# Two expert tiles held back for the last mixing, its norms' halves set side by side, and four steps' exponentials per sum product in the first and last attention

## The chip, the cores and the metric

The kernel runs on 1 core of one Trainium2 chip. The metric is the device time of one execution in microseconds (us), as a median of several. The engines are PE (TensorE: matrix products and transposes), DVE (VectorE), ACT (ScalarE), POOL (GpSimd) and SP (SyncE, which issues most DMAs). Each runs its instructions in the order in which the kernel issued them to it.

## The reference, cut to what matters

One layer for x of shape (4, 256, 32, 32): 4 images, 256 channels, N = 1024 pixels each. A mixing part (`conv`) is followed by a mixture-of-experts part (`ffn`), both added to their input.

```python
def conv(x):                                  # per image
    xn = layernorm(x over channels)
    xm = mamba(4 groups of 64 channels) + skip * xn     # selective scan over N
    g  = sigmoid(conv1d(xm));  R = conv1d(conv1d(g * xm)) + g * xm
    xm2 = conv1d(conv1d(cat(x, R))) + x
    x_local  = conv1d_depthwise(xm2)
    q, k, v  = xm2 @ inw                      # 8 heads of 32
    att = softmax(q @ k.T / sqrt(32))         # 1024 x 1024 per head
    x_global = (att @ v) @ outw
    y  = gelu(layernorm(cat(x_local, x_global) @ fc_w))     # norm "lgn"
    y  = depthwise3x3(layernorm over the pixels(y))         # 9 taps
    return layernorm(y over channels) @ proj_w              # norm "fin"
x = x + conv(ln_c(x))
t = tokens(x)                                 # 4096 x 256
p = top-2 softmax gate(ln_t(t) @ Wg)          # 8 experts
t = t + sum_e p_e * (gelu(ln_t(t) @ W1[e]) @ W2[e])   # 256 -> 1024 -> 256
```

The softmax needs, for each head and query, the sum of the exponentials over all 1024 keys. The norms `lgn` and `fin` need, for each pixel, a mean over the 256 channels.

## The kernel before, in words

**Two parts, one program.** `network()` (lines 73 to 1340) holds the mixing of all four images, the class `Experts` (1352 to 1916) the rest. The order of all work on all engines is written by hand. Each strand of work is a Python generator; `start` puts it among the running ones, `beat` (L1235) advances the tick by one and resumes each strand whose tick has come, and what a strand yields is the number of ticks until its next turn. `until` beats until a flag is set, `drain` until no strand is left. So the yields do not make anything wait on the chip; they fix in which order instructions of different strands stand in each engine's queue. On the chip an instruction waits for the engine's earlier ones and for its operands.

**Images 0 to 2.** The selective scan of an image goes in steps (L592 to 607): a product and a scan on DVE, a product on POOL, sums on PE, 16 steps for each of two halves of N and four groups. The other work of image b-1 (convolutions, attention, joining, norms) and of image b-2 (3x3 taps, final norm, routing) is issued among the scan steps of image b. When the attention of image b-1 starts, no scan step is issued until that attention is three steps from its end (the flag `attended`).

**Image 3.** After the last scan step come, in this order, with expert tiles as filler between: the convolutions of image 3 (L741 on) beside taps, final norm and routing of image 2; the attention of image 3, with no tile beside it (`hold`, L1320); then joining, norms, taps, routing of image 3 with tiles beside it; then the last series of tiles alone.

**Expert tiles.** A tile is 256 rows of one expert's queue, taken through both products. Tiles are sorted into series by which images must have been routed: 8 of image 0 and 1, 8 when image 2 is routed too, 23 when all are; 35 of these 39 run here, the last four only on demand. A tile: a gathered load of its rows `xs` (L1786, SP queue), transposes `xp` (L1832, PE) and a copy `xT` (L1833, DVE), four h steps (products L1855, PE, and two gelus L1860, ACT, each), four y steps (products L1865, PE), then an add of its rows into Y in memory (L1881, POOL queue). The generator `tiles()` (L1148) yields `T["pace"]` ticks after each of the eight steps, 1 if nothing set it. The weights of a tile (2 MB) are loaded two tiles ahead by SP. The first tile of a series also needs the series' table (L1669 to 1740, 22 small operations on DVE). `PACE` (L1273) holds the ticks per tile step for the stages of image 3: joining's products 4, norms 2.2, taps 0.9, routing 2; they are set by `pace()` (L995) only for image 3. While image 3's convolutions run, the pace is 1.

**Attention** (L899 to 982). Four blocks per image (two groups of four heads, two halves of the queries), each of eight steps `kt` of 128 keys. A step: four products of logits `st` (L918, PE, into PSUM), one step ahead of use; four exponentials `e` (L928, ACT, 128 x 512); four products `av` with the values (L960, PE). On odd steps DVE adds the step's four exponentials to those of the step before (L970), and `sum_pair` (L935) sums the pair's rows by four products with ones, behind the next step's `av`. `end_block` (L942) takes the sums' logarithm and its negative exponential on ACT and multiplies on DVE; it is issued in the next block's first odd step, and behind the last step.

**Norms** (`inverse_deviation`, L1000). Per half of the pixels: squares on ACT, a mean over channels on PE (`column_mean`, L371), a root as Ln and Exp on ACT (L355, L356), then one multiplication per channel half on DVE (L1018). ACT's Ln and Exp share one table of functions, gelu and sigmoid need others; a change loads a table (1283 ns in the rows of this profile). `joined` (L1021) calls it for `lgn` behind the products ao and fc, and closes with a gelu; `around` (L1060) has the statistics over pixels, a root, and the 16 taps on DVE (L1097); `sent_off` (L1103) subtracts the means, calls it for `fin`, has the products pr, and routes (`dispatch`, L1503: gate, places in the queues L1567, blank rows written from the ACT queue L1450, rows scattered into XS from the POOL queue L1628).

Of the kernel before, what the change touches and what calls it, by code (L numbers as in the profile page):

```python
# [21 lines left out]
NHEAD, HD = 8, 32  # L22
# [50 lines left out]
def network(  # L73
# [29 lines left out]
    B = x.shape[0]  # L103
# [25 lines left out]
    eps5 = cpool.tile([P, 1], F32, name="eps5")  # L129
# [14 lines left out]
    with tc.tile_pool(name="w_conv", bufs=1) as wp, tc.tile_pool(  # L144
        name="act8", bufs=8
    ) as act8, tc.tile_pool(name="act4", bufs=7) as act4, tc.tile_pool(
        name="act2", bufs=17
    ) as act2, tc.tile_pool(name="steps", bufs=2) as actd, tc.tile_pool(
        name="steps4", bufs=6
    ) as acts, tc.tile_pool(name="rows", bufs=3) as actc, tc.tile_pool(  # L150
        name="small", bufs=1
    ) as small, tc.tile_pool(
        name="spread", bufs=2, space=bass.MemoryType.DRAM
# [107 lines left out]
        ones = experts.every  # L261
# [80 lines left out]
        def half(h):  # L342
            return ts(h, HALF)
# [8 lines left out]
        def root(r, var, eps, scale=1.0):  # L352

            log_exp()
            nc.scalar.activation(r, var, AF.Ln, bias=eps, scale=scale)  # L355
            nc.scalar.activation(r, r, AF.Exp, scale=-0.5)  # L356
# [10 lines left out]
        def column_mean(name, chunks):  # L367

            out = ps(name)
            for ci, chunk in enumerate(chunks):  # L370
                nc.tensor.matmul(  # L371
                    out, ones_mean, chunk, start=(ci == 0), stop=(ci == len(chunks) - 1)
                )
            return out
# [110 lines left out]
        T = {}  # L485
# [374 lines left out]
        NK = N // P  # L860
# [38 lines left out]
        def attention(b):  # L899

            v8, qk = QKV.pop(b)
            rows = [
                largest(b, g, qk[g][:, 0, :], qk[g][:, 1, :]) if shifted else None
                for g in range(2)
            ]
            yield 1
            steps = [(g, h, kt) for g in range(2) for h in range(2) for kt in range(NK)]  # L910

            def logits(g, h, kt):

                q, k = qk[g][:, 0, :], qk[g][:, 1, :]
                sts = [ps(f"st_{b}_{g}_{h}_{kt}_{i}") for i in range(4)]
                for i in range(4):
                    r = ts(i, HD)
                    nc.tensor.matmul(  # L918
                        sts[i], k[r, ts(kt, P)], q[r, half(h)], start=True, stop=not shifted
                    )  # L920
                    if shifted:
                        nc.tensor.matmul(
                            sts[i], ones[HD * i : HD * i + 1, :],
                            rows[g][HD * i : HD * i + 1, half(h)], start=False, stop=True,
                        )
                es = [a2(f"e_{b}_{g}_{h}_{kt}_{i}") for i in range(4)]
                for i in range(4):
                    nc.scalar.activation(es[i], sts[i], AF.Exp, scale=1.0 / HD**0.5)  # L928
                return es

            log_exp()
            ahead = logits(*steps[0])
            pairs, accs, ending = [], [None, None], []

            def sum_pair():  # L935
                kt, acc, es = pairs.pop()
                for i in range(4):
                    nc.tensor.matmul(
                        acc[ts(i, HD)], ones[:, 0:HD], es[i], start=(kt == 1), stop=(kt == NK - 1)
                    )  # L940

            def end_block(g, h, values, total):  # L942

                low, out = a2(f"low_{b}_{g}_{h}"), OT[b][g][:, half(h)]
                at = (2 * b + g) * 2 + h
                keep = [None, None] if shifted else [sums[:, i, at : at + 1] for i in range(2)]
                nc.scalar.activation(low, total, AF.Copy, accum_out=keep[0])
                nc.scalar.activation(low, low, AF.Ln, bias=added)
                nc.scalar.activation(low, low, AF.Exp, scale=-1.0, accum_out=keep[1])
                nc.vector.tensor_tensor(out, values, low, ALU.mult)  # L950

            for at, (g, h, kt) in enumerate(steps):
                es = ahead
                if at + 1 < len(steps):
                    ahead = logits(*steps[at + 1])
                if kt == 0:

                    accs = [ps(f"av_{b}_{g}_{h}_{w}") for w in range(2)]
                for i in range(4):
                    nc.tensor.matmul(  # L960
                        accs[0][ts(i, HD)], v8[:, kt, ts(4 * g + i, HD)], es[i],
                        start=(kt == 0), stop=(kt == NK - 1),
                    )
                if pairs:
                    sum_pair()
                if kt % 2 == 0:
                    first = es
                else:
                    for i in range(4):
                        nc.vector.tensor_tensor(first[i], first[i], es[i], ALU.add)  # L970
                    pairs.append((kt, accs[1], first))
                    if ending:
                        end_block(*ending.pop())
                if kt == NK - 1:
                    ending.append((g, h, *accs))
                if at == len(steps) - 3:
                    T["attended", b] = True
                yield 1
            sum_pair()
            yield 1  # L980
            end_block(*ending.pop())
            yield 1
# [14 lines left out]
            if b == B - 1:  # L997
                T["pace",] = ticks

        def inverse_deviation(name, xc):  # L1000
            r = a4(f"r_{name}")

            def squares(h):
                sq = [a2(f"sq_{name}_{h}_{c}") for c in range(NC2)]
                for c in range(NC2):
                    nc.scalar.activation(sq[c], xc[:, c, half(h)], AF.Square)
                return sq

            for h in range(2):
                sq = squares(h)  # L1010
                yield 1
                var = column_mean(f"var_{name}_{h}", sq)
                yield 2
                root(r[:, half(h)], var, eps5)
                yield 1
            yield 1
            for c in range(NC2):
                nc.vector.tensor_tensor(xc[:, c, :], xc[:, c, :], r, ALU.mult)  # L1018
                yield 1

        def joined(b):  # L1021

            xloc, oT = XLOC.pop(b), OT.pop(b)
            pace(b, PACE["product"])
            xglo = a8(f"xglo_{b}")
            T["attending", b] = True
            yield from in_turn(
                CO_H, lambda at: product(
                    f"ao_{b}_{at[0]}_{at[1]}", aoutT_s, at[0],
                    [oT[ci][:, half(at[1])] for ci in range(NC2)],  # L1030
                ),
                lambda at, r: nc.scalar.activation(
                    xglo[:, at[0], half(at[1])], r, AF.Identity, bias=ob[:, at[0] : at[0] + 1]
                ),
            )

            xc = XC[b] = a8(f"xc_{b}")
            both = (xloc, xglo)
            yield from in_turn(
                CO_H, lambda at: product(  # L1040
                    f"fc_{b}_{at[0]}_{at[1]}", fcT_s, at[0],
                    [both[ci // 2][:, ci % 2, half(at[1])] for ci in range(4)],
                ),
                lambda at, r: nc.scalar.activation(
                    xc[:, at[0], half(at[1])], r, AF.Identity, bias=fcb[:, at[0] : at[0] + 1]
                ),
            )

            T["joining", b] = True
            pace(b, PACE["norm"])  # L1050
            yield from inverse_deviation(f"lgn_{b}", xc)
            for c in range(NC2):
                nc.scalar.activation(
                    xc[:, c, :], xc[:, c, :], AF.Gelu, bias=col("lgn_b", c), scale=col("lgn_w", c)
                )
            loaded[0] = None
            log_exp()
            yield 2

        def around(b):  # L1060
# [17 lines left out]
            xz = []  # L1078
            pace(b, PACE["taps"])
            for c in range(NC2):  # L1080
# [22 lines left out]
        def sent_off(b):  # L1103

            xc = XC.pop(b)
# [12 lines left out]
                lambda h: column_mean(f"mean_{b}_{h}", [xc[:, c, half(h)] for c in range(NC2)]),  # L1118
                centre,
            )  # L1120
            yield from inverse_deviation(f"fin_{b}", xc)

            def residual(at, r):
                co, h = at
# [139 lines left out]
        def until(*flag):  # L1264
            while not T.get(flag):
                beat()
# [3 lines left out]

        PARTS = 2 * NB

        PACE = {"product": 4, "norm": 2.2, "taps": 0.9, "routing": 2, "rows": 0.75}  # L1273
        with tc.manual_schedule(engines=ALL):
            log_exp()
            start(weights(), first_normalised())
# [2 lines left out]
            for b in range(B):  # L1279
                for p in range(PARTS):  # L1280
                    at = b * PARTS + p
                    stop = b > 0 and p == PARTS // 2 - 1 or at == len(parts) - 1
# [33 lines left out]
                flagged(convolutions(B - 1), "convolved"),  # L1316
                one_by_one(around(B - 2), sent_off(B - 2)),
            )
            until("convolved")
            T["hold",] = True  # L1320
            until("held")
            start(flagged(attention(B - 1), "attended", B - 1, 2), local(B - 1))
# [29 lines left out]
class Experts:  # L1352
# [11 lines left out]
    T = 256  # L1364
# [649 lines left out]
```

## Time and profile before

| | us |
|---|---|
| median of three runs | 2473.78 (2473.77 to 2481.73) |
| the profiled execution | 2480.27 |
| its span (first to last instruction) | 2478.3 |
| PE busy, share of the span | 2131.6 (86%) |
| DVE busy | 1631.0 (66%) |
| ACT busy | 1196.3 (48%) |
| POOL busy | 1101.3 (44%) |
| mean granted clock of PE in the span | 0.909 |
| attention of image 0 (506 to 618 us): PE, DVE, ACT busy | 109.6, 70.8, 85.2 of 112 |
| end of the last tile to the end (2441 to 2478.3 us): PE busy | 11.8 of 37.3 |

How to read it: times on the axis are microseconds from the start of the span of one profiled execution. "Busy" is time in which an engine executes instructions other than register, branch, semaphore and DMA-issuing ones; matrix products are pipelined and their ends are modelled, so a fully busy PE need not be at its peak. The granted clock is the share of full speed that the throttle allowed PE. In a line of a timeline the number in brackets is the idle time ahead of an instruction and `<-` what ended it; `xs<-XS` reads "xs, made from XS"; `x8` counts instructions.

A product 512 columns wide stands as two records in PE's counts: 1024 records of `st` are the 512 products of four images.

### The profile page before, as it was taken

The page shows a single profiled execution, that of the slowest core. Times are in us where ns is not written, and L with a number is a line of the kernel's source. Part 1 is how long each engine was busy: PE and PEld are TensorE (multiplying, and loading weights), DVE is VectorE, ACT ScalarE, POOL GpSimd, SP SyncE. Part 2 cuts the span into 40 slices and gives each one's busy share as a digit, 9 for nine tenths or more (in the row PEclk, how much of TensorE's full clock was granted, in tenths as well). Part 3 has the DMA queues.
Part 4 walks back from the last instruction along what each step waited for, and adds up shares of the span by engine and source line. Part 5 has one row for each costly group of instructions (what it writes and reads, how often), then busy time and mean ns, then how long its engine had stood idle before and what let it go on. Part 6 is the DMA issues. An engine that isn't in the chain of part 4 may idle for free. (4 is left out here: it accounts for less than half of the span.)

```text
span 2478.3 us, 28314 instructions
## 1 busy us (share of the span) xinstructions
PE 2131.6 (86%) x8810; PEld 947.8 (38%) x8810; DVE 1631.0 (66%) x2255; ACT 1196.3 (48%) x2020; POOL 1101.3 (44%) x1182
## 2 busy tenths in 40 slices
PE   7777768999978799987689999568999978899995
PEld 2111112322211132222113223115672456788885
DVE  3978998866898978789888787984425254211111
ACT  4554445568655448764264786324238542122221
POOL 0767776622676850465866115561131011322221
PEclk7978988999998899988788999779999988899998
DMA  3534343220343330133422102343330144666665
GB/s 89 140 96 107 95 103 80 58 57 26 77 100 98 74 74 26 35 104 91 124 61 59 46 22 69 88 147 105 112 109 16 58 134 133 194 196 191 195 198 156
DMA packets 154981, 244.31 MB, mean 99 GB/s; under 512 B 34184, under 2 KB 103452, under 8 KB 154816
## 3 DMA queue, kind: packets, MB, share of 16 engines
q1 hardware_dynamic: 135640, 217.05, 30.9%
q0 software_dynamic: 13264, 17.85, 3.7%
q10 hardware_dynamic: 5912, 7.45, 0.9%
q8 instruction: 74, 1.21, 0.2%
q14 instruction: 91, 0.75, 0.1%
HBM read 141.16 MB, written 33.98 MB: 71 GB/s over the span
## 5 line engine op out<-in xcount | busy, mean ns | idle before, releaser
L607 POOL TENSOR_TENSOR hs<-hs,cs 128x512 f32<-128x512 f32 x512 | 670.5, 1311 | 212.2 <-DVE hs L602 166.8
L613 PE MATMUL yp<-hs,quads 128*32 128x512 f32 x1024 | 345.8, 695 | 161.2 <-POOL hs L607 118.9
L588 ACT ACTIVATE dA<-dts,A 128x512 f32<-128x512 f32 x512 | 342.5, 713 | 277.6 <-DMA dts<-dt 189.8
L595 DVE TENSOR_TENSOR dBu<-dts,bs 128x512 f32<-128x512 f32 x512 | 347.7, 679 | 69.6 <-PE bs L580 17.6
L1881 POOL DMA_INDIRECT Y<-ys,dest x70 | 111.0, 1585 | 592.8 <-DVE ys L1875 586.4
L602 DVE TENSOR_TENSOR_SCAN hs<-dA,last,dBu 128x512 f32<-128x512 f32 x256 | 327.6, 1280 | 24.9 <-DVE dBu L595 0.5
L602 DVE TENSOR_TENSOR_SCAN hs<-dA,dBu 128x512 f32<-128x512 f32 x256 | 312.4, 1220 | 31.3 <-ACT dA L588 6.2
L1860 ACT ACTIVATE hs<-h,b 128x256 f32<-128x256 f32 x280 | 117.0, 471 | 398.8 <-PE h L1855 211.3
L928 ACT ACTIVATE e<-st 128x512 f32<-128x512 f32 x512 | 263.2, 606 | 84.8 <-PE st L918 84.5
L1865 PE MATMUL y<-w,hs 128*128 128x256 f32 x1120 | 270.2, 394 | 12.3 <-ACT hs L1860 12.3
L1855 PE MATMUL h<-xT,w 128*128 128x256 f32 x1120 | 254.4, 383 | 1.2 <-DVE xT L1833 1.2
L1865 PEld LDWEIGHTS y<-w,hs 128*128 128x128 f32 x1120 | 219.7, 199 | 55.0 <-ACT hs L1860 14.4
L1833 DVE COPY xT<-xp 128x512 f32<-128x512 f32 x35 | 24.2, 691 | 323.8 <-PE xp L1832 323.7
L606 POOL COPY last<-hs 128x1 f32<-128x1 f32 x256 | 66.9, 261 | 371.8 <-DVE hs L602 340.7
L1855 PEld LDWEIGHTS h<-xT,w 128*128 128x128 f32 x1120 | 214.1, 192 | 41.3 <-issue 10.7
L580 PE MATMUL bs<-u,xpwT_s 128*32 128x512 f32 x1024 | 177.9, 674 | 43.9 <-DVE hs L602 23.8
L613 PEld LDWEIGHTS yp<-hs,quads 128*32 128x32 f32 x1024 | 55.7, 119 | 414.2 <-POOL hs L607 280.8
L970 DVE TENSOR_TENSOR e<-e,e 128x512 f32<-128x512 f32 x256 | 171.2, 730 | 54.1 <-ACT e L928 29.9
L918 PE MATMUL st<-qk 32*128 32x512 f32 x1024 | 193.1, 653 | 6.8 <-DVE hs L602 4.5
L496 PE MATMUL up<-xn,inwk 64*128 64x512 f32 x256 | 138.8, 688 | 11.5 <-DVE hs L602 11.4
L960 PE MATMUL av<-e,v 128*32 128x512 f32 x1024 | 142.6, 621 | 0.0
L918 PEld LDWEIGHTS st<-qk 32*128 32x128 f32 x1024 | 67.6, 187 | 131.9 <-issue 87.6
(273 smaller groups left out, 2511.8 us busy)
## 6 DMA issues: line engine op xcount, KB each, us to landing
w<-in_W_dram SPq DMA_DIRECT2D x136, 512.0 KB
dts<-dt SPq DMA_DIRECT2D x512, 128.0 KB
cs<-cd SPq DMA_DIRECT2D x512, 64.0 KB
xs<-XS SPq DMA_DIRECT2D x35, 260.0 KB
b<-in_b_dram SPq DMA_DIRECT2D x35, 128.0 KB
xn<-in_x_dram SPq DMA_DIRECT2D x8, 512.0 KB
XL<-xl SPq DMA_DIRECT2D x8, 512.0 KB
xl<-XL SPq DMA_DIRECT2D x4, 1024.0 KB
```

The source lines that it names most:

```text
L580: nc.tensor.matmul(bs[r], xpwT_s[:, n, s : s + 1].to_broadcast([P, 32]), T[b, n, "u"][:, half(h)], start=True, stop=True,)
L588: nc.scalar.activation(dA, T[b, n, h, "dts", g][:, 0, :], AF.Exp, scale=A[:, g, n, q : q + 1])
L595: nc.vector.tensor_tensor(dBu, T[b, n, h, "dts", g][:, 1, :], T[b, n, h, "bs", q], ALU.mult)
L602: nc.vector.tensor_tensor_scan(hs, T[b, n, h, "dA", i], dBu, 0.0 if h == 0 else last, ALU.mult, ALU.add)
L607: nc.gpsimd.tensor_tensor(hs, hs, T[b, n, h, "cs", q], ALU.mult)
L613: nc.tensor.matmul(T[b, n, h, "yp"][ts(g, 32)], quads, T[b, n, h, "hs", q * GD + g], start=(q == 0), stop=(q == GS - 1),)
L918: nc.tensor.matmul(sts[i], k[r, ts(kt, P)], q[r, half(h)], start=True, stop=not shifted)
L928: nc.scalar.activation(es[i], sts[i], AF.Exp, scale=1.0 / HD**0.5)
L960: nc.tensor.matmul(accs[0][ts(i, HD)], v8[:, kt, ts(4 * g + i, HD)], es[i], start=(kt == 0), stop=(kt == NK - 1),)
L970: nc.vector.tensor_tensor(first[i], first[i], es[i], ALU.add)
L1855: nc.tensor.matmul(hp[:, i, :], w1(c, k), xT[:, c, :], start=(c == 0), stop=(c == NC2 - 1))
L1865: nc.tensor.matmul(yp[:, ts(t, C)], hs[:, k, ts(t, P)], w2(k), start=(k == 0), stop=(k == NHC - 1))
```

## The change

In the attention of the first and the last image, DVE adds the exponentials of four steps rather than two before one sum product of them, so that a block has two groups of four sum products rather than four; `end_block` keeps its place in the block's step 1. In `inverse_deviation` for image 3 (`alone`), the squares of both halves are issued first, then both column means, then both roots, with a yield ahead of each of these four; for the other images nothing moves. Finally the paces of the tiles for image 3 change, and two are new: 1.6 while image 3's convolutions run (1 before, unset) and 1 again from there to the joining.

```diff
+            many = 4 if b in (0, B - 1) else 2
             def sum_pair():
                 kt, acc, es = pairs.pop()
                 for i in range(4):
                     nc.tensor.matmul(
-                        acc[ts(i, HD)], ones[:, 0:HD], es[i], start=(kt == 1), stop=(kt == NK - 1)
+                        acc[ts(i, HD)], ones[:, 0:HD], es[i], start=(kt < many),
+                        stop=(kt == NK - 1),
                     )
...
-                if kt % 2 == 0:
+                if kt % many == 0:
                     first = es
                 else:
                     for i in range(4):
                         nc.vector.tensor_tensor(first[i], first[i], es[i], ALU.add)
-                    pairs.append((kt, accs[1], first))
-                    if ending:
-                        end_block(*ending.pop())
+                    if kt % many == many - 1:
+                        pairs.append((kt, accs[1], first))
+                if kt == 1 and ending:
+                    end_block(*ending.pop())
...
-        def inverse_deviation(name, xc):
+        def inverse_deviation(name, xc, alone):
             r = a4(f"r_{name}")
...
-            for h in range(2):
-                sq = squares(h)
-                yield 1
-                var = column_mean(f"var_{name}_{h}", sq)
-                yield 2
-                root(r[:, half(h)], var, eps5)
-                yield 1
-            yield 1
+            if alone:
+                sq = [squares(h) for h in range(2)]
+                var = []
+                for h in range(2):
+                    yield 1
+                    var.append(column_mean(f"var_{name}_{h}", sq[h]))
+                for h in range(2):
+                    yield 1
+                    root(r[:, half(h)], var[h], eps5)
+            else:
+                for h in range(2):
+                    sq = squares(h)
+                    yield 1
+                    var = column_mean(f"var_{name}_{h}", sq)
+                    yield 2
+                    root(r[:, half(h)], var, eps5)
+                    yield 1
+                yield 1
...
-            yield from inverse_deviation(f"lgn_{b}", xc)
+            yield from inverse_deviation(f"lgn_{b}", xc, b == B - 1)
...
-            yield from inverse_deviation(f"fin_{b}", xc)
+            yield from inverse_deviation(f"fin_{b}", xc, b == B - 1)
...
-        PACE = {"product": 4, "norm": 2.2, "taps": 0.9, "routing": 2, "rows": 0.75}
+        PACE = {
+            "convolutions": 1.6, "product": 2, "norm": 1.2, "taps": 0.67, "routing": 1.3, "rows": 1
+        }
...
                 one_by_one(around(B - 2), sent_off(B - 2)),
             )
+            T["pace",] = PACE["convolutions"]
             until("convolved")
+            T["pace",] = 1
             T["hold",] = True
             until("held")
```

## The prediction

> **What bounds the kernel now.** I read the 40 slices first, then the busy times by stage, then the engines in order of time where the change acts.
>
> ```profile
> PE   7777768999978799987689999568999978899995
> DVE  3978998866898978789888787984425254211111
> PEclk7978988999998899988788999779999988899998
> ```
>
> A slice is 62 us. DVE carries the scans until slice 27 (1662 us); from there it falls to 2 to 5 and PE carries the time. The stages from 1662 us on (columns: stretch, length, busy PE, PEld, DVE, ACT and POOL with instruction counts, granted clock, DMA share, GB/s):
>
> ```profile
> 1662.00:1735.00 73.00, 65.13 (x220) 39.51 (x221) 40.31 (x56) 38.39 (x52) 11.64 (x13) 0.91 0.40 125
> 1735.00:1854.00 119.00, 119.00 (x496) 86.91 (x494) 41.14 (x118) 32.97 (x64) 24.32 (x33) 1.00 0.38 114
> 1854.00:1942.00 88.00, 88.00 (x642) 26.12 (x643) 47.92 (x74) 73.60 (x146) 10.41 (x15) 1.00 0.06 13
> 1942.00:2099.00 157.00, 136.29 (x504) 98.14 (x503) 64.16 (x165) 61.51 (x101) 18.95 (x19) 0.89 0.38 115
> 2099.00:2165.00 66.00, 51.59 (x231) 44.31 (x230) 12.08 (x43) 11.64 (x28) 27.23 (x40) 0.89 0.70 204
> 2165.00:2441.00 276.00, 275.92 (x1310) 242.56 (x1310) 48.34 (x153) 63.81 (x152) 61.00 (x57) 0.99 0.63 180
> ```
>
> They are: convolutions of image 3 up to its rp products; from there to its attention; its attention; its joining, norms, 3x3 taps and routing; the last held tiles; 19 tiles of the last series. PE is full in the second, third and last, and idles or runs slowly (clock 0.89) in the others. An expert tile costs PE 14.25 us (the transposes xp come every 14.25 us, 2129.56 and 2143.82); that is 8 steps of 1.72 us (8 records of 128x256) and 0.44 us of xp. A 512-wide matmul is two records and costs 0.86 us.
>
> So the time from 1662 to 2165 us is PE work plus PE's losses. Stage 1: 20 tile steps (34.4), 3 xp (1.3), 24 wide matmuls (20.6) = 56 of 72 us, loss 16. Stage 2: 64 us of tiles and 56 of convolutions, routing and projections = 120, no loss. Stage 4 to the places product (2087 us): 45 of dense products and 9.5 half tiles (68) = 113 of 146, loss 33. From there to the xp at 2165 us: 58 of 78, loss 20.
>
> **Two tiles held back.** The order of the two programs shows 7 tiles ahead of attention 3 before and 5 after; at image 3's places product both are at the 12th. Stage 1 loses 8 tile steps, stage 2 one half tile of h and one of y. Stage 2 is full, so it pays 13.8 + 0.4 = 14 us. Stage 1 I followed hop by hop with the durations of its rows: taps of image 2 end at 1691 (one xT copy less), two means and a y step to 1695.5, four gp to 1699; then on ACT sigmoid 1.27, table 1.28, squares 1.15, table, sigmoid, table, root 1.32, table, gelu 0.84, the first depthwise start (1.22) at about 1709 where it was 1723.3; squares, a gelu, the second start to 1717; two DVE passes of 1.28 to 1719.6; rp. It was 1735.6: 16 us. Together 30. The routing and the d4r passes behind rp have fewer tiles to hide under, and I saw no slack check there; I take **-24**. Ends: -14 (only the full stage pays) and -30.
>
> **Where they go.** Stage 4 takes 28.5 us of PE work more. Again hop by hop, from the end of attention, against before's clock times. Three more steps ahead of var_lgn, less a wait of 2.6 us: +3. The norm's "one round trip" is not one on ACT: in the new order a tile's gelu stands ahead of the first root and another between the two, with a table load on each side (1.28 + 0.84 + 1.28 + 1.32 = 4.7 us per half), and the first gelu waits for an h step put behind var_lgn_1. The roots end at 1990 instead of 1982.7: +7.5. Then the bn of the second half stands on DVE behind an xT copy, that behind xp, that behind a y step whose last gelu comes at 1998; and the 22 small DVE operations of the second series' table (4.2 us; before at 1944.6, beside ao) now stand just ahead of the first tap. Taps start +9.5, end +11.6 (2034.8). In the final norm all squares and both roots do stand together, one table load: its multiplication ends +7. Products, rows and gate have 1.5 half tiles more: places +13 (2100).
>
> Behind places it comes back. Before, the eight blank-row DMAs stand on ACT between the 2nd and 3rd gelu of a tile, and PE waits for the third:
>
> ```profile
> 2099.61 10.24 ACTq L1450 DMA_DIRECT2D XS<-blank  x8
> ...
> 2100.81 1.89 PE L1865 MATMUL y<-w,hs 128*128 128x256 f32 x8
> 2110.43 3.78 PE L1865 MATMUL y<-w,hs 128*128 128x256 f32 x8 [7.73 <-ACT hs L1860]
> 2114.01 1.06 PE L1832 MATMUL xp<-ident,xs 128*128 128x128 f32 x4
> 2114.86 4.50 PE L1865 MATMUL y<-w,hs 128*128 128x256 f32 x16
> ...
> 2154.61 3.62 PE L1865 MATMUL y<-w,hs 128*128 128x256 f32 x16
> 2164.91 1.11 PE L1832 MATMUL xp<-ident,xs 128*128 128x128 f32 x4 [6.68 <-DMA xs<-XS]
> ```
>
> After, they stand behind the tile's fourth gelu, and PE has a y half and the next h half (14 us) to run under their 10.2: the 7.7 us go, and 2.8 us of slow matmuls behind them (3.78 for 1.89, 4.50 for 3.62, all that followed to 2119). The 6.7 us before the last series' first xp stay: the table, its register load and the SP queue behind it are ordered as before; POOL's last rows now stand behind the same tile's adds. My sum: xp at 2162.5 instead of 2164.9, -2.4. The path has three PE gaps of 3 to 5 us of its own (y on gelus twice, mean on the last tap); by the 2.8 us after the gap shown I add 5.4 for slow matmuls: **+3** for all behind attention. Ends: -15 (33 us of loss filled by half) and +18 (28.5 less the 10.5, nothing else hidden). The two tiles' weight loads (SP) and adds (POOL) move with them into a stage with DMA share 0.38; the last series runs at 14.25 us a tile with 0.63, which is the cover.
>
> [...]
>
> **Row sums of four.** Per attention 8 of 16 groups of four sum matmuls go, and 32 adds come (0.62 each, 20 us).
>
> ```profile
> 1891.39 4.13 ACT L928 ACTIVATE e<-st 128x512 f32<-128x512 f32 x8 [0.86 <-PE st L918]
> ...
> 1892.30 1.35 PE L918 MATMUL st<-qk 32*128 32x512 f32 x8
> 1893.58 1.06 PE L960 MATMUL av<-e,v 128*32 128x512 f32 x8
> 1894.46 1.04 PE L938 MATMUL av<-e,every 128*32 128x512 f32 x8
> 1895.43 1.14 PE L918 MATMUL st<-qk 32*128 32x512 f32 x8
> 1896.50 1.07 PE L960 MATMUL av<-e,v 128*32 128x512 f32 x8
> ```
>
> A pair of steps takes 5.2 us (av 1891.30 to av 1896.50), the sum group 0.97 of it, while ACT needs 4.13 for the pair and waits 0.86. Without the group a pair is 4.23. A block of eight steps: PE 4 x 5.2 - 2 x 0.97 = 18.9; ACT 32 x 0.516 + 2.2 (end of block) = 18.7. Two equal engines in step lose some: of 8 x 0.97 = 7.8 I take **-5** for image 3. Ends 0 and -7.8. The adds lie under it: DVE goes from 48 to 68 of 83 us. With that cover gone a sum waits on its third add (up to 2.5 us, eight times), and behind it on PE the next logits, for which ACT waits. That is nearer in image 0 (506 to 618 us, the scan stands still until the attention is nearly through): DVE 71 of 112 already, with the next image's norm on it: 91 of 105. I take **-3** there, ends +5 and -7.8.
>
> The norms of images 0 to 2 keep their order; nothing else before 1662 us moves.
>
> **Sum.** -24 + 3 - 5 - 3 = -29 us. The profiled execution took 2480.27 us (span 2478.3 and 2.0 around it), so 2451 against it. It lies 6.5 us above the median of the runs, 2473.78, two of which agree to 0.01 us while the third is 2481.73; the forecast is for the median: **2445**.
>
> **Rivals.**
> 1. The gain is paid back: held tiles do not fit the last mixing. The PE losses there are chain losses (taps 16 x 1.26 on DVE, four tables on ACT), and PE in order makes the chain wait for tiles as much as the reverse. Then -20 in the convolutions, +15 behind attention, -5 and 0: -10, 2464. For: clock 0.89 and PE at 87% there, so each us of tile must hit a gap. Against: the two removed waits at 2102 and 1969.
> 2. The convolutions are chain-bound throughout: only the -14 comes, +3, attentions -2: -13, 2461. For: loss of 16 in stage 1. Against: stage 2's sum fits without any loss.
> 3. Slower: the lgn norm. Gelus and tables stand between its roots; if every tile step until the taps waits like that (three halves more at 4.7 us, and the second series' register load behind the table), the chain grows by 25 rather than 10 and places come at +28; with -14 in front, +3 for half-clock matmuls and -2 for the attentions it is +8 to +15: 2482 to 2489. It decides from about 20 us of growth at the first tap.
> 4. The sums do nothing (DVE late, or ACT the bound): 0 and +5 in place of -8. Shifts each case by 8 to 13, no case alone.
> That the change is not what it says is excluded for sums and tiles, which the order shows; for the lgn norm it holds and is in the forecast.
>
> **Chances.** Forecast 0.62 (2428 to 2458), rival 1 0.15, rival 2 0.13, rival 3 0.10. About 0.5% (12.4 us) is what a measurement can tell from no change: faster below 2461.4. The forecast, a little of rival 1 and half of rival 2 lie there: 0.73; same 0.18; slower 0.09. The range for 8 in 10 takes the forecast's low end, -46 (ends -30, +3, -8, -8, a little inside), and reaches over rivals 1 and 2: 2428 to 2472.
>
> **What would show it.** Attention 3 starts near 1826 us of its span, less what image 0 gained (was 1854.5): under 10 us earlier is rival 2. Attention 3 takes about 83 us from first to last matmul instead of 88; a pair without sums takes 4.3 us. The first tap of image 3 comes 9 to 10 us later after the end of attention than the 58 us of before; over 20 is rival 3. The wait of 7.7 us on gelus behind the blanks is gone; the wait for xs before the last series is still 6 to 7. From the end of attention to that xp: 221 + 5 us (was 223); over 235 is rival 1.

## The result and the profile after

The changed kernel took 2482.32 us (median of 4 runs, 2477.57 to 2484.41) beside 2475.35 us for the kernel before (4 runs): ratio 1.0021, 95% interval 0.9997 to 1.0044. In a second measurement on another occasion it took 2475.92 beside 2481.28 us: 0.9968 (0.9947 to 0.9989). Taken together the change makes no difference that can be told from zero. The forecast of 2445 us was 37 us below the first measurement and 31 below the second; both lie above its range of 2428 to 2472.

The kernel before itself took medians from 2473.78 to 2481.40 us on the occasions of this study, and single runs from 2470.83 to 2489.41; the first three runs, two of which agreed to 0.01 us, did not show that spread. The profiles show that much of it lies outside the change: all but the four stretches below took 1715.6 to 1730.8 us in fourteen profiles of the kernels of this study. The two lowest, 1715.6 and 1717.6, are those of the two executions with the highest mean granted clock, 0.918 and 0.917; in the others it was 0.904 to 0.912. So the stretches that the change does touch are compared one by one, and the whole time last.

The profiled execution of the changed kernel took 2481.32 us, its span 2479.4. These are its slices of 62 us, the rows that answer to those of the kernel before:

```profile
PE   7777778999977799987689999658999889899995
DVE  3979998887899887789978787985537154211111
PEclk7978888999988899998689999768999999899998
```

And its stages after the scans (columns as before: stretch, length, busy PE, PEld, DVE, ACT and POOL with counts, granted clock, DMA share, GB/s): convolutions to the rp products, from there to attention 3, attention 3, mixing and routing, the last held tiles, 19 tiles of the last series.

```profile
1669.00:1730.00 61.00, 52.42 (x155) 28.33 (x156) 37.24 (x48) 31.16 (x42) 8.19 (x8) 0.86 0.33 107
1730.00:1836.00 106.00, 105.61 (x421) 74.69 (x419) 39.90 (x110) 32.83 (x57) 27.31 (x42) 0.98 0.39 115
1836.00:1926.00 90.00, 88.97 (x578) 24.90 (x576) 66.95 (x106) 73.11 (x145) 5.37 (x6) 0.98 0.09 25
1926.00:2101.00 175.00, 155.63 (x642) 118.13 (x642) 68.59 (x174) 68.59 (x117) 25.25 (x25) 0.95 0.42 121
2101.00:2163.00 62.00, 51.06 (x229) 43.99 (x227) 13.33 (x51) 11.53 (x28) 27.23 (x41) 0.93 0.75 214
2163.00:2439.00 276.00, 275.69 (x1304) 242.55 (x1305) 48.20 (x152) 63.81 (x152) 61.25 (x57) 0.99 0.63 181
```

The first two stages are 12 and 13 us shorter. The third, attention 3, is not shorter at all, though DVE works 19 us more in it. The fourth is 18 us longer as it is cut here. What was won ahead of attention 3 is gone at its end and in the mixing.

Four stretches, read from the first and last instructions named, hold what the change touches. A: first logits of attention 0 to the last scan step of image 1. B: last scan step of image 3 to the first logits of attention 3. C: attention 3 from its first to its last av product. D: from there to the first xp of the last series. "Rest" is the span less the four. It holds the time from the first logits of attention 3 to its first av product as well, which was 4.0 to 4.1 us in runs 2, 3 and 4 and in the first profile of the changed kernel, and 1.9 in the other ten profiles, the second one of the changed kernel among them.

| kernel | A | B | C | D | rest | ratio to the kernel before (95%) |
|---|---|---|---|---|---|---|
| before, two profiles | 245.8, 247.1 | 198.1, 198.0 | 84.2, 84.1 | 224.9, 224.9 | 1725.4, 1726.9 | 1 |
| changed, two profiles | 252.2, 252.7 | 173.5, 173.5 | 84.5, 84.0 | 238.4, 238.5 | 1730.8, 1726.3 | 1.0021 (0.9997 to 1.0044), 0.9968 (0.9947 to 0.9989) |
| 1 sums alone | 252.2 | 198.2 | 84.0 | 218.5 | 1722.4 | 1.0026 (1.0009 to 1.0042) |
| 2 changed, sums of two | 245.8 | 173.2 | 84.7 | 239.1 | 1726.6 | 0.9973 (0.9957 to 0.9990) |
| 3 changed, table early | 252.3 | 177.0 | 84.4 | 229.6 | 1727.1 | 0.9962 (0.9944 to 0.9979) |
| 4 changed, old norm | 252.2 | 173.5 | 84.5 | 235.2 | 1726.7 | 0.9995 (0.9982 to 1.0008) |
| 5 table early, sums of four in the last attention only | 246.9 | 176.7 | 84.0 | 230.8 | 1721.2 | 0.9910 (0.9887 to 0.9932) |
| 6 changed, sums a step later | 250.5 | 173.3 | 80.7 | 238.0 | 1715.6 | 0.9960 (0.9947 to 0.9974) |
| 7 table early, old norm | 252.1 | 173.4 | 84.0 | 228.3 | 1717.6 | 0.9954 (0.9937 to 0.9970) |
| 8 before, tiles held back alone | 246.9 | 176.7 | 84.2 | 249.2 | 1720.6 | 1.0007 (0.9995 to 1.0019) |
| 9 as 5, sums a step later | 246.9 | 173.3 | 80.7 | 232.0 | 1720.5 | 0.9919 (0.9899 to 0.9940) |
| 10 as 9, old norm | 247.0 | 176.8 | 80.7 | 230.2 | 1727.5 | 0.9928 (0.9911 to 0.9945) |

Kernels with the same code up to attention 3 show B at 173.3 or 176.8 (rows 9 and 10), so 3.5 us of B is chance; A, C and D repeat to within about 1.3 us in the kernels run twice. The change is then +6.0 in A, -24.5 in B, 0 in C and +13.5 in D: -5 us in all, which lies between the +7.0 and the -5.4 of the two measurements.

### The profile page after: what moved, and what is told of

It is laid out like the page before. It is cut to its first block, busy times and chain, and to the rows that moved or that the text cites. A ratio compares the mean times of both kernels' runs of the same rounds, so it can differ in the third digit from the quotient of the medians.

```text
span 2479.4 us, 28218 instructions
## 1 busy us (share of the span) xinstructions
PE 2138.2 (86%) x8682; PEld 944.9 (38%) x8682; DVE 1676.6 (68%) x2319; ACT 1195.0 (48%) x2019; POOL 1103.6 (45%) x1182
## 5 line engine op out<-in xcount | busy, mean ns | idle before, releaser
L602 DVE TENSOR_TENSOR_SCAN hs<-dA,last,dBu 128x512 f32<-128x512 f32 x256 | 327.6, 1280 | 24.5
L975 DVE TENSOR_TENSOR e<-e,e 128x512 f32<-128x512 f32 x320 | 212.5, 729 | 26.3 <-PE av L965 22.1
L580 PE MATMUL bs<-u,xpwT_s 128*32 128x512 f32 x1024 | 183.1, 694 | 42.0 <-DVE hs L602 24.0
L918 PE MATMUL st<-qk 32*128 32x512 f32 x1024 | 201.2, 656 | 8.2 <-DVE hs L602 4.5
L496 PE MATMUL up<-xn,inwk 64*128 64x512 f32 x256 | 149.5, 734 | 10.9 <-DVE hs L602 10.8
```

Source lines behind the costliest of these rows:

```text
L496: nc.tensor.matmul(up, inwk[rows, c, k, :], XN[b][rows, c, ds(k + h * HALF, HALF)], start=(k == 0), stop=(k == KC - 1),)
L580: nc.tensor.matmul(bs[r], xpwT_s[:, n, s : s + 1].to_broadcast([P, 32]), T[b, n, "u"][:, half(h)], start=True, stop=True,)
L602: nc.vector.tensor_tensor_scan(hs, T[b, n, h, "dA", i], dBu, 0.0 if h == 0 else last, ALU.mult, ALU.add)
L918: nc.tensor.matmul(sts[i], k[r, ts(kt, P)], q[r, half(h)], start=True, stop=not shifted)
```

## The experiments

**Is it the sums?** Two kernels, one with the sums alone, one with all but the sums.

Run 1, the kernel before with these lines and the others of the change's first block:

```diff
-                        acc[ts(i, HD)], ones[:, 0:HD], es[i], start=(kt == 1), stop=(kt == NK - 1)
+                        acc[ts(i, HD)], ones[:, 0:HD], es[i], start=(kt < many),
+                        stop=(kt == NK - 1),
...
-                if kt % 2 == 0:
+                if kt % many == 0:
```

> The kernel before with the row sums of four steps alone (images 0 and 3); norms and paces as before. Theory (the sums cost time: with 12 adds in a row a sum waits on DVE, and PE's next logits wait behind it): attention of image 0, first to last av step, about 103 us instead of 99.5; that of image 3 82 to 83 instead of 82.9; the time 3 to 5 us above the kernel before. Rival (the forecast: half of the removed sums comes back; what was seen in the changed kernel is chance): 8 us below the kernel before.

Measured: 2481.96 beside 2477.38 us, ratio 1.0026. Attention 0 took 102.9 us from its first to its last av step where it had taken 99.5, attention 3 81.8 where it had taken 82.9. Behind attention 0, from the last av step to the end of A, it took 141.9 us where it had taken 139.4. With 0.6 us ahead of the first av step A grew by 6.5. Those 0.6 are chance: the second profile of the kernel before has them too, and its attention 0 took 100.2. The 139.4 and the 141.8 to 142.0 stand in all seven profiles with sums of two and all seven with sums of four. DVE, busy 124.4 of the 138.3 us behind the attention of the kernel before, has eight adds among the first scan steps in place of four, first in the kernel before, then in the changed one:

```profile
613.09 3.55 DVE L970 TENSOR_TENSOR e<-e,e 128x512 f32<-128x512 f32 x4
```

```profile
621.82 3.56 DVE L975 TENSOR_TENSOR e<-e,e 128x512 f32<-128x512 f32 x4
...
627.23 3.54 DVE L975 TENSOR_TENSOR e<-e,e 128x512 f32<-128x512 f32 x4
```

The theory holds for image 0; in image 3 the last av products take 0.9 us longer, so that only 0.2 of the 1 us between the starts of the steps reaches C. D came out at 218.5 us, 6.4 below the kernel before, with the same order of instructions there; the measured median agrees with a D of 225 (+6.5 in A) and not with 218.5. The profiled execution, 2477.14 us, was the second fastest of the nine, 4.8 us below their median, so its D need not be that of the others; this stays open (see the last section).

Run 2, the changed kernel with:

```diff
-            many = 4 if b in (0, B - 1) else 2
+            many = 2
```

> The changed kernel with the sums of two steps again everywhere; norms and paces stay changed. Theory (the sums cost time): image 0's attention back to 99.5 us from 102.9, the time 3 to 5 us below the changed kernel. Rival (the sums gain): 8 us above it. In both the start of attention 3 stays some 24 us earlier after the last scan step than in the kernel before.

Measured: 0.9973; A back at 245.8 us, C and D as in the changed kernel, B 173.2. The rival, 8 us above the changed kernel, is out: the ratio lies at the lower of the changed kernel's two, 1.0021 and 0.9968. That the whole time is shorter without the sums these ratios do not show; A, 6.4 us shorter, does.

Why the sums gain nothing in attention 3 is seen in one block of the changed kernel. The timeline of all engines, about its second block (the columns as before):

```profile
1863.12 2.50 DVE L975 TENSOR_TENSOR e<-e,e 128x512 f32<-128x512 f32 x4 [0.38 <-PE av L965]
...
1869.76 7.30 DVE L975 TENSOR_TENSOR e<-e,e 128x512 f32<-128x512 f32 x12
...
1873.17 1.06 PE L965 MATMUL av<-e,v 128*32 128x512 f32 x8
...
1874.05 1.71 PE L942 MATMUL av<-e,every 128*32 128x512 f32 x8
...
1875.69 1.14 PE L918 MATMUL st<-qk 32*128 32x512 f32 x8
...
1876.85 2.07 ACT L928 ACTIVATE e<-st 128x512 f32<-128x512 f32 x4 [1.52 <-PE st L918]
```

The adds of the block's second step are done by 1865.6 us. Behind them in DVE's order stands the closing product of the block before, which waited for ACT until 1869.15, and only then come twelve adds in a row, 7.3 us: those of the third, fourth and sixth steps (the fifth step's exponentials begin the next four). The eight that the sum needs end at 1874.66. The sum products take PE 1.71 us where they took 1.04, because the last of the four waits for the last of these adds, and the logits stand behind them, so ACT waits 1.52 us for the logits. Step by step, from one av product to the next, a block took 2.92, 2.77, 3.54, 2.07, 2.92, 2.28, 2.92, 2.28 us before and 2.92, 2.77, 3.30, 2.22, 3.59, 2.28, 2.07, 2.27 after: of the two sums that went, the one in the third step was hidden by ACT's end of block (0.24 gained), the one in the seventh gives its 0.85, and the fifth step gives 0.67 back and the fourth 0.15. A block took 21.70 us and takes 21.42.

**Is it that the sum comes too early for its adds?** Run 6, the changed kernel with:

```diff
-                if pairs:
+                if pairs and (many == 2 or kt % many == 1):
                     sum_pair()
```

> The changed kernel with one edit: a sum of four steps is issued behind the second step after its last one rather than the first, so that its adds have a step more. Theory (PE stands at the sum until DVE has the third add, and the logits behind it wait): the step that holds the sum falls from 3.59 to some 2.3 us in attention 3 and from 5.57 to some 3 in image 0's third block, a block of attention 3 from 21.4 to 20.5 us, image 0's stretch from 252.2 to 246 to 249, the time 4 to 8 us below the changed kernel. Rival (DVE's 32 more adds themselves hold up what is behind them in image 0): the steps as said in attention 3, image 0 within 1 us of 252.

Measured: in attention 3 the fifth and sixth steps take 2.07 and 3.04 us in place of 3.59 and 2.28, a block 20.53, C 80.7 us. That is as expected. A fell only to 250.5, above the theory's 246 to 249 and below the rival's 252: by this one profile, where A repeats to 1.3 us, the wait at the sum is 1.7 us of it and the larger part is something else. In attention 3 of this kernel the sum stands behind the sixth step's av, and by then its adds are done:

```profile
1852.78 9.71 DVE L975 TENSOR_TENSOR e<-e,e 128x512 f32<-128x512 f32 x16
...
1858.25 1.18 PE L965 MATMUL av<-e,v 128*32 128x512 f32 x8
1859.13 1.16 PE L942 MATMUL av<-e,every 128*32 128x512 f32 x8
```

The sum follows av at once and takes 1.16 us instead of 1.71. In image 0 DVE is busy 213 us of A's 252 (191 of 246 before): the 20 us of adds fill idle time for the most part, but some 4 us stay in A even with the later sum.

**Where did D grow?** The waits of PE between attention 3 and the last series, first in the kernel before, then in the changed one (columns: who waited for what, us in total, times, longest):

```profile
PE y L1865 <- ACT hs L1860: 12.3, 4, 7.7
PE xp L1832 <- DMA xs<-XS: 6.7, 1, 6.7
PE mean L371 <- DVE xi L1097: 4.7, 1, 4.7
PE var_fin L371 <- ACT sq_fin L1006: 4.1, 1, 4.1
```

```profile
PE xp L1853 <- DMA xs<-XS: 17.8, 3, 6.8
PE y L1886 <- ACT hs L1881: 7.2, 2, 3.9
PE mean L371 <- DVE xi L1114: 2.5, 1, 2.5
```

The wait of 7.7 us on gelus behind the blank rows is gone, as forecast, and the waits at `mean` and `var_fin` are smaller. But PE now waits three times for a tile's rows rather than once. The first of these is for the first tile of the second series. SP's own row in the changed kernel, from the end of attention 3 to 2010 us, names what held that load:

```profile
SPq L1822 <- DVE taken L1753: 29.7, 1, 29.7
```

and the timeline shows where it lands:

```profile
1995.08 0.17 DVE L1753 TENSOR_SCALAR taken<-starts 128x8 f32<-128x8 f32 x1
...
1995.65 0.92 SPq L1833 DMA_DIRECT2D w<-in_W_dram  x2
...
2006.70 1.12 PE L1853 MATMUL xp<-ident,xs 128*128 128x128 f32 x4 [6.51 <-DMA xs<-XS]
...
2007.86 0.69 DVE L1854 COPY xT<-xp 128x512 f32<-128x512 f32 x1 [5.76 <-PE xp L1853]
```

SP reads the number of the expert whose weights it has to load from the table, so it stands from 1965 to 1995 us until DVE has worked the table out. The weights and the rows of the tile start only then, PE waits 6.51 us at xp, and DVE 5.76 us at the copy behind it, with the other eleven of the 16 taps queued behind the copy. The taps take 33.0 us from the first to the last where they took 23.7.

Run 3, the changed kernel with the table two tiles ahead of its place (`load` then only uses it):

```diff
+                if n == 5:
+                    tables.append(experts.series(1, temp))
                 hs = act8.tile([P, NHC, experts.T], F32, tag="a8", name=f"hs_{n}")
```

> The changed kernel with one edit: the second series' table (22 small DVE operations) is issued two tiles earlier, just behind attention 3, where it lay before; the loads that read it keep their place. Theory (SP stands on that table for 30 us, so the rows of the series' first tile come late, PE waits 6.5 us for them, DVE's copy of them waits, and the 3x3 taps wait behind that copy): the wait for xs at 2006.7 us goes, the taps take 24 to 27 us instead of 33.0, from the end of attention 3 to the last series' first xp 228 to 232 us instead of 238.4, the time 6 to 10 us below the changed kernel. Rival (PE has to put 28 us of tiles there in any case, and the wait only moves): taps shorter, but the stretch to that xp still 236 to 240, the time within 2 us.

Measured: ratio 0.9962; the taps take 28.4 us, D 229.6. PE's waits in D become

```profile
PE xp L1855 <- DMA xs<-XS: 12.5, 2, 7.6
```

The wait at that tile is gone and D is 8.8 us shorter, where the rival had it within 2 us of the changed kernel's 238.4: that much of D was the table. The whole time alone does not show it: the ratio cannot be told from the lower of the changed kernel's two, 0.9968, and the profile's B is 3.5 us longer by chance. Run 7 and run 5, measured beside the changed kernel, do (below). The taps missed the expectation by 1.4 us (two waits of DVE for xp, 2.8 and 1.8 us, remain).

**Is the new norm order worth anything?** Run 4, the changed kernel, and run 7, run 3's kernel, each with:

```diff
-            if alone:
+            if False:
```

> The changed kernel with the norms of image 3 half by half again; sums and paces stay changed. Theory (a tile's gelu stands between the two roots all the same, with four table loads, so the new order gains nothing): from the end of attention 3 to the first tap 66 to 74 us (70.9 in the changed kernel), the time within 3 us of the changed kernel. Rival (the round trip saved is worth a wait of a norm): first tap 5 us later or more, the time 5 us above it.

> The changed kernel with the second series' table issued just behind attention 3 and with image 3's norms half by half again. Theory (PE's waits set the stretch behind attention 3, and the waits for rows are most of them: 17.8 of 30.6 us in the changed kernel, 13.6 of 27.0 with the old norm alone): from the end of attention 3 to the last series' first xp 226 to 231 us, 4 to 9 less than the 235.2 of the old norm without the table. Rival (the new norm order is what makes the table's edit pay): 235 or more.

Measured: run 4, first tap 81.0 us behind the last av product where the changed kernel had 70.9, but D 235.2, 3.2 us less, and ratio 0.9995. Run 7, D 228.3, ratio 0.9954. The expectation for the first tap in run 4 failed, the rival's 10 us are there; yet neither D nor the time follows it. The chain of the norm is later and the stretch is not longer, so the first tap does not set D: in run 4 the places product comes 12.2 us later than in the changed kernel, and from it to the last series' xp PE takes 54.4 us where it took 69.8, since one tile more is under way ahead of it (its xp is issued before the places product, not behind). In run 7 the table's gain under the old order is 6.9 us of D beside 8.8, and the time is 6.4 us below the changed kernel's on the same occasion, so the gain does not hang on the new order.

**What do the two tiles alone do?** Run 8, the kernel before with:

```diff
+            T["pace",] = 1.6
             until("convolved")
+            T["pace",] = 1
```

> The kernel before with one edit: pace 1.6 while image 3's convolutions run, 1 again up to the joining. Sums, norms and all other paces as before. Theory (the shorter stage is worth 24.6 us, and what the new paces behind attention 3 bring is that the two tiles fill PE's waits there): last scan step to attention 3 173.5 us; behind it the two tiles stand after the places product, where PE is nearly full, so the stretch from the end of attention 3 to the last series' first xp grows by 20 to 28 from its 218 to 225, and the time is within 5 us of the kernel before. Rival (the old paces have room as well): the stretch grows by less than 15, the time 10 us or more below the kernel before.

Measured: ratio 1.0007; B 176.7, D 249.2. The theory holds: 21 to 25 us leave B and 24.3 come back in D, all of two tiles' 28.5 but 4. The new paces and norms behind attention 3 bring D from 249.2 to 238.4, so they do fill waits, 11 us of them (14 with the old norm, run 4); with the table in time (D 229.6 in run 3) 20 of them.

**Do the costs add?** Run 5, the changed kernel with run 3's edit and

```diff
-            many = 4 if b in (0, B - 1) else 2
+            many = 4 if b == B - 1 else 2
```

> The changed kernel with two edits: sums of four in the last attention only, and the second series' table issued just behind attention 3. Theory (the two costs found are separate and add): 6.5 us from image 0 and 8.8 from the table, 15 us below the changed kernel, 15 to 19 below the kernel before. Rival (PE has the work to do in any case; one of the two was chance): 6 to 9 us below the changed kernel.

Measured: 2460.21 beside 2481.28 us, ratio 0.9910; against the changed kernel on the same occasion 15.7 us less. A 246.9 and D 230.8: they add. Runs 9 and 10 add run 6's later sums to it, run 10 with the old norm as well.

> The changed kernel with sums of two in image 0, the second series' table just behind attention 3, and the last attention's sums of four issued a step later. Theory (the three parts add): attention 3 from first to last av step 80.7 us instead of 84.0, image 0's stretch 245.8 to 247, from the end of attention 3 to the last series' first xp 229 to 231, the time 18 us below the changed kernel, some 20 to 25 below the kernel before. Rival (a shorter attention 3 only makes the rows behind it wait longer): as the kernel without the late sums, 15 below the changed kernel.

> The kernel of the run before in this list with image 3's norms half by half. Theory (the order of the norm's halves moves PE's waits and not their sum): the first tap 4 to 10 us later behind attention 3, the stretch to the last series' first xp and the time within 3 us of the one with the new order. Rival (the new order is worth its round trip): 4 us or more slower.

Measured: run 9 2457.36 beside 2481.40 us, 0.9919; C 80.7, D 232.0. Run 10 2463.02, 0.9928; first tap 7.9 us later, D 230.2. Run 9's 3.3 us in C are there, and D is 1.1 longer; the intervals of runs 5 and 9 overlap, so whether the later sums shorten the whole time is not settled. Runs 5 and 9 beat both kernels, by 0.8 to 0.9% of the kernel before.

**Two kernels run again.** The changed kernel and the kernel before:

> The changed kernel once more, beside the next three on one chip. Theory (stage by stage: 24.6 us less between the last scan step and attention 3, 6.5 more in and around image 0's attention, 2 more at the start of attention 3, 1 less in it, 13.5 more behind it): 3 to 4 us below the kernel before. Rival (the first measurement holds): 5 us above it. Its attention of image 0 and all behind it, to the last scan step of image 1, takes 252.2 us as in every kernel with sums of four there, where those with sums of two take 245.8.

> The kernel before once more, for its stages in a second profile beside the next three. Theory (the stretches are the program's, the scans and PE's granted clock vary from run to run): last scan step to attention 3 198 us, attention 3 84.0 to 84.2, image 0's stretch 245.8, each within 1 us; from the end of attention 3 to the last series' first xp between 218 and 225 us, with the same waits of PE (12 us on gelus, 6 to 7 on rows) in both and a higher clock in the shorter. Rival (225 belongs to the program): 224 to 226 again.

Measured: the changed kernel 0.9968, the other side of the first measurement, A 252.7 and D 238.5. The kernel before: 2483.02 us (one run), B 198.0, C 84.1, D 224.9. The theory that D ranges from 218 to 225 by chance found no support; D repeated to 0.1 us, with much the same waits.

## Why the prediction was wrong

The forecast was -29 us; the stretches give -5. Of the 24 us between them 9 lie in the first attention's row sums, 5 in the last one's, and 10.5 behind attention 3, of which 8.8 are the second series' table. These are the failed steps: adds taken to lie under PE and ACT because DVE has room on average, and a table priced at DVE's time alone.

**The convolutions: right.** -24 forecast, -24.6 and -24.5 measured in B (-21 in the kernels that show B at 176.7 to 177.0). Of its parts the first stage gave 12.7 us (last scan step to rp 79.8, then 67.1) where the working had 16, the second 11.9 where it had 14. The 6 us taken off were the right size partly by luck: they were meant for the routing and the d4r passes behind rp, and over half of the shortfall lies ahead of rp.

**Row sums in the last attention: the size failed.** -5 forecast, 0 measured. The step "the adds lie under it: DVE goes from 48 to 68 of 83 us" holds as a sum (67 of 90) and fails as a schedule. A wait "on its third add" was named, and priced at nothing because DVE has room on average; it comes once in every block, since the adds of the third and fourth steps stand behind the closing product of the block before. The working's blocks were too short as well: it took all four pairs of steps at 5.2 us, 20.8 a block, where the kernel before took 21.70, because ACT's end of block lengthens the third step; a sum product removed there gains 0.24. With the sum one step later, run 6 shows 3.5 of the 5 us.

**Row sums in the first attention: the sign failed.** -3 forecast with an upper end of +5, +6.0 measured. The argument "91 of 105" counted only the stretch in which the scans stand still. The scans behind it need DVE next. By the second profile of the kernel before some 3 us of the loss lie in the attention and 2.4 behind it; run 6 puts 1.7 of them down to the wait at the sum, and for the rest the extra adds are the likely cause, since A is back at 245.8 to 247.1 in every kernel without them.

**Behind attention 3: the mechanism was right up to the first tap.** Forecast and measured growth, from the last av product: the end of the lgn norm's roots, and so its multiplication, +7.5 and +6.9, the first tap +9.5 and +11.4. Then the last tap +11.6 and +20.8, the places product +13 and +21.5. The failed step is the second series' table, whose 22 small DVE operations "now stand just ahead of the first tap", priced at their own 4.2 us. What reads the table was left out: SP, and through it the weights, the rows, xp, the copy xT and the taps behind that on DVE. The table's register load was named only in rival 3, as an addition to the chain. This cost 8.8 us: with the table early (run 3) the places product stands at +12.5 and D at +4.7, beside +13 and +3 forecast (D +5.9 and +7.1 in runs 5 and 9).

**Behind the places: right in kind.** The gelu wait of 7.7 us went, as said, though ACT still stands for 10.94 us on the blank rows. In the changed kernel PE has work meanwhile, and then waits for rows of the next tile but one:

```profile
2103.57 10.99 ACTq L1471 DMA_DIRECT2D XS<-blank  x8
...
2114.65 2.30 ACT L1881 ACTIVATE hs<-h,b 128x256 f32<-128x256 f32 x6 [10.94 <-DMA XS<-blank]
...
2124.94 1.11 PE L1853 MATMUL xp<-ident,xs 128*128 128x128 f32 x4 [4.40 <-DMA xs<-XS]
...
2163.31 1.12 PE L1853 MATMUL xp<-ident,xs 128*128 128x128 f32 x4 [6.84 <-DMA xs<-XS]
```

The stretch from places to xp fell by 7.9 us. The forecast's own clock times, places at 2100 and xp at 2162.5, had it fall by 15.4, with 5.4 us for slow matmuls set aside for the whole of D; 4.40 us of new wait are more than the 2.1 us missing if these 5.4 are counted here, and part of the 7.5 if not. In the kernel before, the DMA engines stood idle from about 2114 to 2118 us (0 GB/s), behind that gelu wait; in the changed one they moved 331 GB/s from 2106 to 2126 us, so the new wait looks like the same bytes met without the pause. That is read from two traces only; no run here took the blank rows away.

**The norm: right that a gelu stands between its roots, wrong that its chain sets the time.** On ACT the second root starts 4.8 us behind the first, with two table loads and a gelu between, beside 4.7 in the working. But runs 4, 7 and 10 show D 1 to 3 us shorter with the old order although the first tap is 8 to 10 us later.

**The rivals and the range.** Rival 1 ("the gain is paid back") gave +15 behind attention 3 and rival 4 gave 0 and +5 for the sums; both numbers came true together, and D, 238.4, lies over the 235 that was named as the sign of rival 1. Its cause was not rival 1's: that had the chain wait for tiles and the tiles for the chain, and run 3 shows a table worked out too late for the load that reads it. The working had the rivals shift one another by 8 to 13 us and then gave the range for each alone. Together, with -24 in the convolutions, they make -4 us, beside the -5 of the stretches. (The low end of the range was to lie a little inside the sum of the ends, -30, +3, -8 and -8; these make -43, and the range takes -46.) The forecast then fell a further 6.5 us by setting the profiled execution against a median of three runs; on the three later occasions the kernel before had medians of 2477 to 2481 us.

## What to carry to other kernels

An engine's share of busy time says that work fits, not that it is done when the next engine asks: before adding work to it, find the instruction that waits for the last of that work and give it a step of room. When a small calculation is moved, follow the slowest thing that reads it; here a queue read a table and a whole tile's loads stood behind that read for 29.7 us. Filling a stage with work from another pays only for the waits it really meets, and when two rivals do not exclude each other the range must hold both at once.

## What the runs showed of the hardware

The same wait is followed by slow products in one profile and by fast ones in another. Behind the 2.60 us wait ahead of `var_lgn`, 16 y products took 4.77 us in the kernel before (granted clock 0.75 from 1974.4 to 1979.0 us) and 3.62 in run 1, where nothing differs in the order of that stage; behind the places product 5.99 (0.60 from 2088.1 to 2093.9) and 3.67. These two places make up over half of the 6.4 us between D of 224.9 and 218.5, and the granted clock in three parts of the stage was 0.93, 0.86 and 0.87 before and 0.96, 0.89 and 0.90 in run 1. In the kernel before it was 0.50 from 2110.4 to 2114.2 us, behind the 7.73 us wait on gelus, and eight y products took 3.78 us there where the eight ahead of the wait took 1.89; in run 1 they took 3.78 too, behind 7.98 us. No run shows why the products behind one and the same wait are slow in one execution and not in the other: a difference by chance would fit two executions, but D of the kernel before repeated to 0.1 us in a second profile, so it stays open. Summing slow products as a cost of each gap, as the forecast did with 5.4 us, is then an estimate good to some 6 us at best in this stretch.
